# A four-layer network on one core: table loads in the planner's costs, a feature bias per 128 tokens, and a layernorm split off

## The chip, the core and the metric

The kernel runs on one core of a Trainium2 chip. The core has five engines, each with a queue of its own that it works through in order: PE (TensorE, matrix products), DVE (VectorE), ACT (ScalarE, activation functions), POOL (GpSimd), and SP (SyncE, which here only starts transfers). They wait for each other by semaphores. The metric is the device time of one execution in microseconds (us); less is better.

## The reference

2048 tokens of 128 features pass through four transformer layers, each an attention and a network, each behind a layernorm and added to the stream `x`. All data are fp32.

```python
x = x + L0_attn(ln(x))     # 16 heads of 64, softmax over all keys
x = x + L0_ffn(ln(x))      # 8 experts, top 1, capacity T/8
x = x + L1_attn(ln(x))     # 16 heads, causal
x = x + L1_ffn(ln(x))      # mixing with the token before, see below
x = x + L2_attn(ln(x))     # reduces to one 128x128 product
x = x + L2_ffn(ln(x))      # ternary weights, relu
x = x + L3_attn(ln(x))     # 16 heads, region mask, feature bias
x = x + L3_ffn(ln(x))      # binarised weights, gelu
```

Two parts matter here. The mixing (L1_ffn), for normed x with `x_prev` the same rows one token earlier:

```python
xr = mu_r * x + (1.0 - mu_r) * x_prev
xk = mu_k * x + (1.0 - mu_k) * x_prev
r = sigmoid(xr @ W_r);  k_act = square(relu(xk @ W_k))
out = r * (k_act @ W_v)
```

The feature bias of L3_attn, one number for each query token and head:

```python
hmid = gelu(x @ ext_w1 + ext_b1)                  # 5 features of 64
feature_scores = sigmoid(hmid . ext_w2 + ext_b2)  # 5 per token
bias = feature_scores @ softmax(faw).T            # [token, head]
attn = softmax(dots + bias)                       # bias along the query only
```

## The kernel before

The stream `x` stays on the chip for the whole run. A turned copy of its normed rows, `xT`, feeds the products. An attention layer runs over 8 pairs of heads; within a pair over 8 groups of 256 queries. For a group, PE makes scores in strips of 32 queries (L498), DVE moves each strip out of PSUM and takes row minima (`scan`, L508; the scores are made with the opposite sign), POOL and ACT gather the minima and hand them out as a shift (L554 to L568; in L3 POOL takes the bias off and adds it again on the way, L561 and L562), ACT does the exponentials (L580), DVE turns the result (L607), PE weighs the values (L639) and projects (L697), ACT divides (L707), POOL adds to `x` (L725).

Nothing of this is ordered by hand. Every piece of work is a `Step` with an engine, an estimated cost in us, what it comes after, and which buffers it takes. `run` (from L119) is a list scheduler: it simulates the five engines with the estimated costs and, again and again, gives out the step that can start first. On each engine the key (a tick, then the place) sets the preference; a later step goes ahead of a preferred one that still has to wait if, by the estimate, it ends within 0.1 us of the time at which that one can start (L147). The order in which the steps are given out is the order of the instructions in each engine's queue; at run time no engine passes over an instruction that waits. So an estimated cost changes no instruction, but it can change every queue behind it. Before the change a step has one fixed cost; some costs carry a part for loading activation tables, such as 2.6 for the sigmoids (L1147, L1239) and 1.9 for the first Gelu of a chunk (L1225). ACT holds one set of function tables at a time; the exponential, the sigmoid and the Gelu of this kernel are in different sets, and the compiler puts an ACT_TABLE_LOAD where the order changes from one to another.

Buffers come from rings. `MISC` is a ring of three PSUM banks (named `t` in the profile), used by almost everything but scores and weighing; `MID`, `MIXED` and `PAIRED` are rings of four, three and two SBUF tiles. A step that takes a buffer waits for the readers of the one that it replaces.

Between the first (L1) and the last (L3) of the attention layers that matter here lie, for each of five spans of tokens (three of 512, two of 256): the mixing (`rest`: a layernorm, the inputs xk and xr on ACT and DVE, L1096 to L1101, products L1130, L1105 and L1109, sigmoid L1147), a layernorm and the one product of L2's attention (`attend`, L1113), a layernorm and the ternary network (`feed_forward`, products L981 and L1003), and a layernorm for L3. Then for each chunk of 512 tokens the keys, queries and values of L3 (L392, L413) and the feature bias (`features`): three products and Gelus (L1220, L1225), a product and the sigmoid (L1233, L1239), and the weighing of the five features for 16 heads. L3 needs the keys of all tokens for its first scores.

The bias is wanted per strip: POOL reads `bias[0:Q]` (Q is 32) for the 32 queries of a strip, while DVE's minima sit on 128 partitions. In `features` before, POOL copies each strip of the scores four times side by side (L1247), one matmul makes the bias of one strip on all 128 partitions (L1254, 16 in a chunk), and DVE copies the result of four strips at a time (L1260). `bias` has 128 partitions, of which the readers use the first 32.

A layernorm (`normalise`, from L236) is statistics on DVE (L243 to L245), a power on POOL (L248 to L250), the scaling spread over ACT (L253), POOL or DVE (L258), a turn on PE (L264) and a copy on ACT (L279). The column of `xT` of the last token of a span is kept in `edge` (L1117) for the span behind it, in two columns used by turns, so that a new one waits for the readers of the old one.

Of the kernel before, what the change touches and what calls it, by code (L numbers as in the profile page):

```python
# [16 lines left out]
P = 128  # L17
# [41 lines left out]
def network(ctx: ExitStack, tc: tile.TileContext, a: dict, out: bass.AP):  # L59
# [18 lines left out]
    class Ring:  # L78


        def __init__(self, pool, name, shape, bufs, ordered=True):
            self.bufs, self.takers, self.held, self.ordered = bufs, [], [], ordered
            self.make = lambda: pool.tile(list(shape), F32, tag=name, name=name, bufs=bufs)
            rings.append(self)

    class Held:


        def __init__(self, ring):
            self.ring, self.users = ring, []  # L90

    class Step:
        def __init__(self, key, engine, us, do, after=(), takes=(), uses=(), then=None):
            self.key, self.engine, self.us, self.do, self.takes = key + (len(steps),), engine, us, do, takes
            self.after, self.order, self.then, self.end = list(after), [], then, None
            for h in takes:
                h.by = self
                h.users.append(self)
                h.ring.takers.append(self)
            for h in uses:  # L100
                self.after.append(h.by)
                h.users.append(self)
            steps.append(self)
# [15 lines left out]
    def run():  # L119
# [14 lines left out]
        open_, free, next_ = [[] for _ in range(5)], [0.0] * 5, [None] * 5  # L134
        for s in steps:
            if not s.left:
                open_[s.engine].append(s)
        for _ in range(len(steps)):
            best = None
            for e in range(5):  # L140
                found = None
                for s in [next_[e]] if next_[e] else sorted(open_[e], key=lambda s: s.key):
# [4 lines left out]
                    if found is None or t + s.us <= found[0] + 0.1:  # L147
# [8 lines left out]
            s.end = free[e] = start + s.us  # L156
            for h in s.takes:
                h.t = h.ring.make()
# [77 lines left out]
    def normalise(add, t0, n, after, before=(), row=None, hurry=False):  # L236


        mv, xn, pt = Held(MEANS), Held(NORMED), Held(MISC)
# [128 lines left out]
    class Pair:  # L368
# [19 lines left out]
        def projected(self, add, c, to, which, s, takes):  # L388
            pp, b = Held(MISC), self.layer.biases[which]
# [18 lines left out]
        def valued(self, add, c):  # L408
            pv, v = Held(MISC), self.v[c]
# [7 lines left out]
            made = add(PE, 0.8, make, self.layer.ready[c], takes=[pv, v], uses=[self.w])  # L417
# [19 lines left out]
    class Group:  # L437
# [104 lines left out]
        def spread_lowest(self, add, add_later, j, found):  # L542
# [16 lines left out]
            def with_bias():  # L559
                to, b = first().rearrange("p (h i) -> p h i", h=2), self.biases(j)[0:Q]  # L560
# [15 lines left out]
        def exps(self, add, j, h, part, shifted):  # L576
# [15 lines left out]
            return add(ACT, us, do, [shifted], takes=[self.sums] if first else [], uses=uses)  # L592
# [60 lines left out]
        def sum_up(self, add, made):  # L653

            ps, r = Held(MISC), Held(SHARES)
# [32 lines left out]
        def project_out(self, tick, weighed, r):  # L688

            y, pair, oT = [Held(MISC) for h in range(2)], self.pair, self.oT  # L690
# [88 lines left out]
    def output_bias(add):  # L779
        wo, pr = Held(DOUBLE), Held(MISC)  # L780
# [27 lines left out]
    def folded(add):  # L808
        q2T, av = [Held(MID) for k in range(4)], Held(MID)
        pb, pa, pt, pw = (Held(MISC) for k in range(4))  # L810
# [44 lines left out]
    moe_w = Held(DOUBLE)  # L855
# [4 lines left out]
    def experts(add, t0, after):  # L860

        r, pl, pc, pp, pb, pickT = Held(ROUTES), Held(MISC), Held(MISC), Held(MISC), Held(MISC), Held(PAIRED)
# [60 lines left out]
        made = add(ACT, 0.25, lambda: nc.scalar.activation(at(PROBS), at(PROBS), AF.Exp), [made], uses=[r])  # L923
# [10 lines left out]
        for i in range(4):  # L934
            pe, parts = [Held(MISC) for half in range(2)], Held(PAIRED)
# [37 lines left out]
    def feed_forward(add, t0, n, after, full, w1T, b1, func, w2T):  # L973

        hT, made, po = [Held(MID) for f in range(NC)], [], Held(MISC)
        for f in range(0, NC, 2):
            ph = [Held(MISC) for k in range(2)]
# [17 lines left out]
            for k in range(2):  # L995
                made.append(
                    add(ACT, wide(P * n), lambda k=k, f=f, ph=ph: act(f + k, ph[k]), uses=[ph[k], hT[f + k]])
# [14 lines left out]
        add(PE, 0.55 * n, second, made, takes=[po], uses=hT)  # L1012
# [8 lines left out]
    edge = keep([P, 2], "edge")  # L1021
    rests = [keep([P, 1], n) for n in ("rest_r", "rest_k")]
    ternary_w = Held(DOUBLE)

    def ternary(add):
# [14 lines left out]
        for i in range(2):  # L1040
            tot, g, half, less = (keep([P, 1], f"{n}{i}") for n in ("tot", "g", "half", "less"))
            pg, low = Held(MISC), Held(MID)
# [44 lines left out]
    edges = []  # L1087

    def rest(add, t0, n, after, hurry, made):
        m = P * n  # L1090
        xr, xk, ka, r = Held(MIXED), Held(MIXED), Held(MIXED), Held(PAIRED)
        pk, pr, pv, po = (Held(MISC) for k in range(4))
        xs, own = x[:, t0 : t0 + n, :], len(edges) % 2

        def parts(to, part):
            nc.scalar.mul(to.t[:, 1:m], xT[:, bass.ds(PAD + P * t0, m - 1)], part)  # L1096
            before = edge[:, 1 - own : 2 - own] if t0 else xT[:, PAD - 1 : PAD]
# [13 lines left out]
        def attend():  # L1111
            for i in range(n):
                nc.tensor.matmul(pv2.t[:, bass.ts(i, P)], lhsT=xT[:, cols(t0 + i)], rhs=w2, start=True, stop=True)  # L1113

        done, _ = normalise(add, t0, n, after, L1_read(t0, n), hurry=hurry)
        kept = add(
            DVE, 0.15, lambda: nc.vector.tensor_copy(edge[:, own : own + 1], xT[:, bass.ds(PAD + P * (t0 + n) - 1, 1)]),  # L1117
            [done] + (edge_read[-1] if edge_read else []),
        )
        read, mixed = [kept], []  # L1120
        for to, part, mu in ((xk, rests[1], mu_k), (xr, rests[0], mu_r)):
            s = add(ACT, 0.3 + wide(m), lambda to=to, part=part: parts(to, part), [done] + edges[-1:] + made, takes=[to])
            mixed.append(add(DVE, 0.1 + 0.00125 * m, lambda to=to, mu=mu: mix(to, mu), [s], uses=[to]))
            read += [s, mixed[-1]]
        edge_read.append(read[1::2])
        edges.append(kept)
# [9 lines left out]
        add(PE, 0.2 * n, receive, mixed[1:2], takes=[pr, r], uses=[xr])  # L1136
# [9 lines left out]
            2.6 + wide(m),  # L1146
            lambda: nc.scalar.activation(r.t[:, 0:m], pr.t[:, 0:m], AF.Sigmoid),  # L1147
            uses=[pr, r],
        )
        add(PE, 0.2 * n, gate, [square], takes=[pv], uses=[ka])  # L1150
# [17 lines left out]
        pv2 = po  # L1168
        attended = add(PE, 0.2 * n, attend, [done, w2_made], takes=[po])
# [16 lines left out]
    edge_read, bu_added, ob_added = [], [], [[] for c in range(4)]  # L1186

    def L1_read(t0, n):
        return L1.readers[t0 // 4]
# [3 lines left out]
    bias = keep([P, T // Q, H], "bias")  # L1193
# [3 lines left out]
    def feature_weights(add):  # L1197

        pf = Held(MISC)
# [7 lines left out]
        made = add(ACT, 0.25, lambda: nc.scalar.activation(fw, faw, AF.Exp, bias=fw_top), [made])  # L1207
# [4 lines left out]
    def features(add, c):  # L1212

        hm, made = [Held(MID) for j in range(3)], []
        fs, pf = Held(MIXED), Held(MISC)
        for j in range(3):
            n, ph = P if j < 2 else DH, Held(MISC)
# [10 lines left out]
            made.append(add(ACT, 0.6 if j else 1.9, act, uses=[ph, hm[j]]))  # L1228

        def score():  # L1230
# [6 lines left out]
        add(PE, 1.85, score, made, takes=[pf, fs], uses=hm)  # L1237
        scored = add(
            ACT, 2.6, lambda: nc.scalar.activation(fs.t[0:NF, :], pf.t[0:NF, :], AF.Sigmoid, bias=eb2),  # L1239
            uses=[pf, fs],  # L1240
        )
        for k in range(4):
            some, pbias = Held(PAIRED), Held(MISC)

            def spread(k=k, some=some):
                strips = fs.t[0:NF, :].rearrange("p (g q) -> p g q", q=Q)[:, 4 * k : 4 * k + 4, :]
                nc.gpsimd.tensor_copy(  # L1247
                    some.t[0:NF, :].rearrange("p (g c q) -> p g c q", c=4, q=Q),
                    strips.unsqueeze(2).to_broadcast([NF, 4, 4, Q]),
                )  # L1250

            def weigh(some=some, pbias=pbias):
                for i in range(4):
                    nc.tensor.matmul(  # L1254
                        pbias.t[:, bass.ts(i, H)], lhsT=some.t[0:NF, bass.ts(i, P)], rhs=fwT, start=True, stop=True
                    )

            def copy(k=k, pbias=pbias):
                to = bias[:, bass.ds(16 * c + 4 * k, 4), :].rearrange("p t h -> p (t h)")
                nc.vector.tensor_copy(to, pbias.t[:, 0 : 4 * H])  # L1260

# [173 lines left out]
```

## Time and profile before

| | us |
|---|---|
| median of 3 runs (3492.92 to 3493.73) | 3493.64 |
| the profiled execution | 3494.28 |
| its span, first to last instruction | 3492.6 |
| PE busy | 3397.9 (97%) |
| DVE busy | 3211.9 (92%) |
| ACT busy | 2807.6 (80%) |
| POOL busy | 965.4 (28%) |

The profile shows one execution. The times of the text are us from the start of its span. A matmul in fp32 shows up as two records, so 64 matmuls are 128. A line such as L1254 is a line of the kernel before.

The rows of the page for the parts that the change touches give, before a bar, the busy us and the mean ns of one, and after it the idle time of the engine just before, with what ended it:

```profile
L580 ACT ACT_TABLE_LOAD x10 | 12.8, 1283 | 0.2
L990 ACT ACT_TABLE_LOAD x5 | 6.4, 1283 | 0.1
L1225 ACT ACT_TABLE_LOAD x4 | 5.1, 1283 | 8.5 <-PE t L1220 6.5 <-issue 1.9
L1239 ACT ACT_TABLE_LOAD x4 | 5.1, 1283 | 0.1
L1147 ACT ACT_TABLE_LOAD x3 | 3.8, 1283 | 0.1
```

With one at the very start there are 27 table loads, 27 times 1283 ns or 34.6 us of ACT. The rows of the bias are 128 records of L1254 on PE (21.3 us busy), 16 copies of L1247 on POOL (9.5 us) and 16 of L1260 on DVE (3.3 us).

### The profile page before, as it was taken

The page shows a single profiled execution, that of the slowest core. Times are in us where ns is not written, and L with a number is a line of the kernel's source. Part 1 is how long each engine was busy: PE and PEld are TensorE (multiplying, and loading weights), DVE is VectorE, ACT ScalarE, POOL GpSimd, SP SyncE. Part 2 cuts the span into 40 slices and gives each one's busy share as a digit, 9 for nine tenths or more (in the row PEclk, how much of TensorE's full clock was granted, in tenths as well). Part 3 has the DMA queues.
Part 4 walks back from the last instruction along what each step waited for, and adds up shares of the span by engine and source line. Part 5 has one row for each costly group of instructions (what it writes and reads, how often), then busy time and mean ns, then how long its engine had stood idle before and what let it go on. Part 6 is the DMA issues. An engine that isn't in the chain of part 4 may idle for free. (4 is left out here: it accounts for less than half of the span.)

```text
span 3492.6 us, 115619 instructions
## 1 busy us (share of the span) xinstructions
PE 3397.9 (97%) x47018; PEld 1844.2 (53%) x47018; DVE 3211.9 (92%) x8019; ACT 2807.6 (80%) x8709; POOL 965.4 (28%) x2837
## 2 busy tenths in 40 slices
PE   8999999999999899999999988899999999999998
PEld 3545454554545455655555654455555555555555
DVE  8999999999999889989999883699999999999996
ACT  6888888888888667888888975578888888888886
POOL 2122222212222353232323344222222222222233
PEclk9999999999999899999999998899999999999999
DMA  1000000000000000000000000000000000000000
GB/s 47 2 5 2 5 5 2 5 2 5 5 2 5 1 5 8 6 6 6 6 6 6 6 2 4 4 5 5 2 5 2 5 4 4 5 2 2 2 5 10
DMA packets 22961, 19.00 MB, mean 5 GB/s; under 512 B 3556, under 2 KB 21612, under 8 KB 22426
## 3 DMA queue, kind: packets, MB, share of 16 engines
q1 hardware_dynamic: 22362, 11.55, 1.2%
q8 instruction: 368, 6.03, 0.7%
q14 instruction: 167, 1.37, 0.1%
q0 software_dynamic: 64, 0.06, 0.0%
HBM read 10.60 MB, written 1.05 MB: 3 GB/s over the span
## 5 line engine op out<-in xcount | busy, mean ns | idle before, releaser
L580 ACT ACTIVATE e<-e,shift 128x512 f32<-128x512 f32 (+14 forms) x3072 | 1973.9, 648 | 28.2 <-POOL shift L568 20.1
L508 DVE TENSOR_SCALAR_CACHE_REDUCE e<-s 128x512 f32<-128x512 f32 (+15 forms) x3072 | 1659.0, 589 | 99.5 <-PE s L498 98.5
L498 PE MATMUL s<-kT,qT 64*32 64x512 f32 (+8 forms) x24576 | 1458.4, 534 | 22.3 <-DVE e L508 22.3
L607 DVE STREAM_TRANSPOSE e<-e 128x2048 f32<-128x2048 f32 (+10 forms) x768 | 1435.2, 1871 | 9.3 <-ACT e L580 8.9
L639 PE MATMUL o<-e,v 128*64 128x256 f32 (+1 forms) x10496 | 1270.2, 374 | 6.1 <-DVE e L607 4.3
L639 PEld LDWEIGHTS o<-e,v 128*64 128x64 f32 x10496 | 748.3, 137 | 545.3 <-issue 297.7
L498 PEld LDWEIGHTS s<-kT,qT 64*32 64x32 f32 x24576 | 416.5, 105 | 518.8 <-issue 215.9
L580 ACT ACTIVATION_READ_ACCUMULATOR e<-e,shift 128x1 f32 x3072 | 591.3, 192 | 0.0
L554 POOL COPY low<-low 32x8 f32<-32x8 f32 x1152 | 211.3, 183 | 1182.6 <-DVE e L508 1144.1
L725 POOL TENSOR_TENSOR x<-x,part 128x256 f32<-128x256 f32 x384 | 281.1, 732 | 267.0 <-ACT part L707 251.7
L568 ACT COPY shift<-shift 32x8 f32<-32x8 f32 x768 | 149.9, 195 | 140.9 <-POOL shift L562 88.8
L707 ACT ACTIVATE part<-t,r 128x128 f32<-128x128 f32 x768 | 218.2, 367 | 43.9 <-PE t L697 36.2
L508 DVE DVE_READ_ACCUMULATOR e<-s 128x1 f32 x3072 | 230.9, 75 | 0.0
L392 PE MATMUL t<-xT,w 128*128 128x512 f32 x384 | 213.6, 647 | 3.7 <-ACT xT L279 3.5
L680 POOL TENSOR_TENSOR r<-r,inverse 128x4 f32<-128x4 f32 x128 | 130.5, 1020 | 304.4 <-ACT r L683 303.7
L712 ACT COPY oT<-o 128x256 f32<-128x256 f32 x192 | 70.7, 368 | 162.2 <-PE o L639 162.1
L639 PE MATMUL o<-e,va 128*64 128x128 f32 x1024 | 195.5, 273 | 0.0
L498 PE MATMUL s<-beyond,eye 64*32 64x32 bf16 x2560 | 159.9, 176 | 0.0
L697 PE MATMUL t<-w,oT 64*128 64x128 f32 x1536 | 139.8, 299 | 0.5 <-ACT xT L279 0.3
L697 PEld LDWEIGHTS t<-w,oT 64*128 64x128 f32 x1536 | 102.3, 187 | 67.9 <-issue 24.6
L639 PEld LDWEIGHTS o<-e,va 128*64 128x64 f32 x1024 | 126.0, 137 | 0.0
L498 PEld LDWEIGHTS <-regions 64*32 64x32 bf16 x1024 | 65.6, 93 | 113.4 <-issue 79.4
(187 smaller groups left out, 2107.3 us busy)
## 6 DMA issues: line engine op xcount, KB each, us to landing
w<-in_L_wq SPq DMA_DIRECT2D x24, 64.0 KB, 1.9
w<-in_L_wk SPq DMA_DIRECT2D x24, 64.0 KB, 2.2
w<-in_L_wv SPq DMA_DIRECT2D x24, 64.0 KB, 2.0
w<-in_L_wo SPq DMA_DIRECT2D x24, 64.0 KB, 2.1
x<-in_x SPq DMA_DIRECT2D x4, 256.0 KB, 4.7
out_x<-x SPq DMA_DIRECT2D x3, 256.0 KB, 2.3
big<-in_L_wo SPq DMA_DIRECT2D x1, 512.0 KB
big<-in_moe_w SPq DMA_DIRECT2D x1, 512.0 KB
```

The source lines that it names most:

```text
L392: nc.tensor.matmul(pp.t, lhsT=self.w.t[:, which, :], rhs=xT[:, cols(4 * c, 4)], start=True, stop=True)
L498: nc.tensor.matmul(s[h].t[on, bass.ds(first, size)], lhsT=lhsT, rhs=rhs, start=m == 0, stop=m == len(terms) - 1,)
L508: nc.vector.tensor_scalar(self.e(h)[:, i, 0:n], s.t[:, 0:n], 1.0, None, ALU.mult, ALU.min, accum_out=self.lows[j].t[:, 0, 4 * h + i % 4 : ...
L554: nc.gpsimd.tensor_copy(low.t[0:Q, c], low.t[bass.ts(c, Q), 0])
L568: (nc.gpsimd.tensor_copy if causal else nc.scalar.copy)(shift.t[bass.ts(c, Q)], first())
L580: nc.scalar.activation(e, e, AF.Exp, bias=self.shifts[j].t[:, 4 * h + i % 4 : 4 * h + i % 4 + 1], scale=-1.0, accum_out=self.sums.t[:, h, ...
L607: nc.vector.transpose(rows()[:, :, 0:n], rows()[:, :, 0:n])
L639: nc.tensor.matmul(self.o.t[bass.ds(DH * h, DH), i0:i1, :], lhsT=lhsT, rhs=self.e(h)[:, i0:i1, bass.ts(t, Q)], start=t == 0, stop=t == las ...
L680: nc.gpsimd.tensor_tensor(some, some, inverse, ALU.pow)
L697: nc.tensor.matmul(y[h].t[:, bass.ts(j, P)], lhsT=oT.t[half, bass.ts(j, P)], rhs=pair.w.t[half, 3, :], start=True, stop=True,)
L707: nc.scalar.mul(part.t[:, j, :], y[h].t[:, bass.ts(j, P)], r.t[:, j, h : h + 1])
L725: POOL, 0.74, lambda part=part: nc.gpsimd.tensor_tensor(xs, xs, part.t, ALU.add), [divided], uses=[part]
```

## The change

Three things. The planner keeps the set of tables that ACT would hold and adds 1.3 us to a step that needs another one (`us(s)`); the steps with Exp, Sigmoid and Gelu say which they need, and the parts for tables leave their fixed costs. With this, some other costs are set anew (values 0.8 to 1.0, blocks of 128 in the mixing 0.2 to 0.26, the second product of a network 0.55 to 0.93 per block, `score` 1.85 to 2.8). The feature bias is made for 128 tokens in one matmul, with the tokens on the partitions, and four copies bring the four strips to the first 32 partitions; POOL's copies and 12 of 16 matmuls of a chunk are gone. The mixing's first layernorm is added as steps of its own, all five ahead of the rest, and each span has its own column of `edge`. Tiles also get names of their own in the profile (a product of the bias is `pbias` now, not `t`).

```diff
+        table = None
+
+        def us(s):
+            return s.us + (1.3 if s.table and s.table != table else 0.0)
...
-                    if found is None or t + s.us <= found[0] + 0.1:
+                    if found is None or t + us(s) <= found[0] + 0.1:
...
-            s.end = free[e] = start + s.us
+            s.end = free[e] = start + us(s)
+            table = s.table or table
...
-            made = add(PE, 0.8, make, self.layer.ready[c], takes=[pv, v], uses=[self.w])
+            made = add(PE, 1.0, make, self.layer.ready[c], takes=[pv, v], uses=[self.w])
...
-            return add(ACT, us, do, [shifted], takes=[self.sums] if first else [], uses=uses)
+            return add(ACT, us, do, [shifted], takes=[self.sums] if first else [], uses=uses, table=AF.Exp)
...
-        add(PE, 0.55 * n, second, made, takes=[po], uses=hT)
+        add(PE, 0.93 * n, second, made, takes=[po], uses=hT)
...
-    edge = keep([P, 2], "edge")
+    edge = keep([P, NT], "edge")
...
+    def first_norm(add, t0, n, after, hurry):
+        done, _ = normalise(add, t0, n, after, L1.readers[t0 // 4], hurry=hurry)
+        last = t0 + n - 1
+        to, some = edge[:, last : last + 1], xT[:, bass.ds(PAD + P * (t0 + n) - 1, 1)]
+        kept[t0 + n] = add(DVE, 0.15, lambda: nc.vector.tensor_copy(to, some), [done])
+        return done
...
-        done, _ = normalise(add, t0, n, after, L1_read(t0, n), hurry=hurry)
-        kept = add(
-            DVE, 0.15, lambda: nc.vector.tensor_copy(edge[:, own : own + 1], xT[:, bass.ds(PAD + P * (t0 + n) - 1, 1)]),
-            [done] + (edge_read[-1] if edge_read else []),
-        )
-        read, mixed = [kept], []
+        read, mixed = [kept[t0 + n]], []
+        needs = [done] + made + ([kept[t0]] if t0 else [])
...
-            2.6 + wide(m),
+            wide(m),
             lambda: nc.scalar.activation(r.t[:, 0:m], pr.t[:, 0:m], AF.Sigmoid),
             uses=[pr, r],
-        )
-        add(PE, 0.2 * n, gate, [square], takes=[pv], uses=[ka])
+            table=AF.Sigmoid,
+        )
+        add(PE, 0.26 * n, gate, [square], takes=[pv], uses=[ka])
...
-    bias = keep([P, T // Q, H], "bias")
+    bias = keep([Q, T // Q, H], "bias")
...
-            made.append(add(ACT, 0.6 if j else 1.9, act, uses=[ph, hm[j]]))
+            made.append(add(ACT, 0.6, act, uses=[ph, hm[j]], table=AF.Gelu))
...
-        add(PE, 1.85, score, made, takes=[pf, fs], uses=hm)
+        def weigh():
+            for i in range(4):
+                nc.tensor.matmul(
+                    pbias.t[:, bass.ts(i, H)], lhsT=fs.t[0:NF, bass.ts(i, P)], rhs=fwT, start=True, stop=True
+                )
+
+        def copy():
+            for q in range(4):
+                to = bias[:, bass.ts(c, 16), :].rearrange("p (t i) h -> p i t h", i=4)[:, q]
+                nc.vector.tensor_copy(to, pbias.t[bass.ts(q, Q), 0 : 4 * H].rearrange("p (t h) -> p t h", h=H))
+
+        add(PE, 2.8, score, made, takes=[pf, fs], uses=hm)
         scored = add(
-            ACT, 2.6, lambda: nc.scalar.activation(fs.t[0:NF, :], pf.t[0:NF, :], AF.Sigmoid, bias=eb2),
-            uses=[pf, fs],
-        )
-        for k in range(4):
-            some, pbias = Held(PAIRED), Held(MISC)
-
-            def spread(k=k, some=some):
-                strips = fs.t[0:NF, :].rearrange("p (g q) -> p g q", q=Q)[:, 4 * k : 4 * k + 4, :]
-                nc.gpsimd.tensor_copy(
-                    some.t[0:NF, :].rearrange("p (g c q) -> p g c q", c=4, q=Q),
-                    strips.unsqueeze(2).to_broadcast([NF, 4, 4, Q]),
-                )
...
-            made = add(POOL, 0.6, spread, [scored], takes=[some], uses=[fs])
-            add(PE, 0.8, weigh, [made, fwT_made], takes=[pbias], uses=[some])
-            L3.biased[c].append(add(DVE, 0.16, copy, uses=[pbias]))
+            ACT, 0.6, lambda: nc.scalar.activation(fs.t[0:NF, :], pf.t[0:NF, :], AF.Sigmoid, bias=eb2), uses=[pf, fs],
+            table=AF.Sigmoid,
+        )
+        add(PE, 0.7, weigh, [scored, fwT_made], takes=[pbias], uses=[fs])
+        L3.biased[c].append(add(DVE, 0.5, copy, uses=[pbias]))
...
+    mix_spans = [(0, 4), (4, 4), (8, 4), (12, 2), (14, 2)]
     spans = [(0, 4), (4, 4), (8, 4), (12, 2), (14, 2)]
...
-    for t0, n in spans:
-        rest(planner(L1.left(t0, n)), t0, n, L1.outputs(t0, n) + [bu_added[t0 // 4]], n < 4, made)
+    done = {}
+    for t0, n in mix_spans:
+        done[t0] = first_norm(
+            planner(L1.left(t0, n)), t0, n, L1.outputs(t0, n) + [bu_added[t0 // 4]], n < 4
+        )
+    for t0, n in mix_spans:
+        rest(planner(L1.left(t0, n)), t0, n, done[t0], n < 4, made)
```

## The prediction

> **What bounds the kernel now.** I cut the span where the character of the work changes and read the windows view of these stretches (columns: busy us of PE, PE's weight loads, DVE, ACT, POOL, then granted clock, DMA share, GB/s):
>
> ```profile
> 1400.00:2000.00 600.00, 593.01 (x11755) 358.09 (x11746) 544.66 (x1977) 512.48 (x1931) 184.86 (x706) 1.00 0.02 6
> 2000.00:2150.70 150.70, 132.40 (x1468) 81.35 (x1467) 108.56 (x338) 107.01 (x292) 68.07 (x141) 0.91 0.01 2
> 2150.70:2230.60 79.90, 60.06 (x248) 38.91 (x250) 22.98 (x94) 32.29 (x66) 25.73 (x46) 0.81 0.02 7
> 2230.60:2270.40 39.80, 35.30 (x429) 14.48 (x429) 38.01 (x93) 29.17 (x80) 10.39 (x43) 0.87 0.01 2
> 2270.40:3370.00 1099.60, 1098.85 (x14662) 588.63 (x14670) 1076.04 (x2253) 908.23 (x2702) 283.46 (x873) 1.00 0.01 3
> ```
>
> In the attention layers PE has no gap to speak of (593 of 600, 1098.9 of 1099.6): there a microsecond of PE work is a microsecond of time, and work of the other engines is free while it fits. At 2230 to 2270, where the third attention layer (L3) opens, DVE is the bound (38.0 of 39.8). The change works mostly in 2000 to 2230, the mixing and the ternary network. PE is busy 132 of 151 us at a clock of 0.91 while the attention layer before (L1) ends, and 60 of 80 us at 0.81 in the tail behind its last weighing (the last L639 of L1 ends at 2150.7; the first scores of L3 start at 2230.6). No engine is full in the tail; it is one chain from token span to token span. So I read the chain of waits there, in order of time (start us, us, what):
>
> ```profile
> 2129.89 6.56 PE t L1254 x32
> 2136.46 2.01 PE t L1130 x2
> ...
> 2181.53 2.08 PE t L392 x2
> 2183.61 6.93 PE t L1254 x32
> 2190.54 1.15 PE t L1130 x2
> ...
> 2275.47 0.99 PE t L1254 x8
> ...
> 2289.94 3.80 PE t L1254 x32
> ```
>
> L1254 is `weigh`, the feature bias; each fp32 matmul is recorded as two, so 16 matmuls of a chunk are 32 records. All four chunks show up on PE, and two full batches stand on the path of the stretch that has no other bound.
>
> **The feature bias, per 128 tokens.** It removes, per chunk of 512 tokens, 4 POOL spreads and 12 of 16 matmuls with a 128x16 result; the 4 DVE copies of 64 elements a partition remain, on 32 partitions (now 211 ns each, and I keep that: free in either form). The spreads, 16 of 604 ns, 9.5 us, cost nothing now: POOL is busy 28% of the span, and PE was always late enough for them. The matmuls I price by batch.
> (a) Chunk 0: 6.56/32 = 205 ns a record. 8 records are 1.64 us: **-4.9 us**. Next late would be L1130, whose input was mixed by 2126.0, and the last weighing of L1, whose last transpose ended at 2131.6: both were ready inside the batch, so PE passes the gain on.
> (b) Chunk 1: 6.93 to 1.73 us, -5.2. The L1130 behind it had its input from the mix at 2177.89 (0.49 us) and only queued. The changed order issues the two receiving matmuls (L1105, 0.85 us) ahead of the bias, in a gap; but ACT now makes both mixing inputs before the sigmoid, 0.8 us later for the x transpose. **-5.3 us**.
> (c) Chunks 2 and 3: 24 records of chunk 2 ran at 2245, while DVE was the bound: nothing. The other 0.99 us and the 3.80 of chunk 3 lie where PE is the bound again. The 8 records that chunk 3 keeps are 0.95 at 119 ns: **-3.8 us**. Two of its three L1220 matmuls also move ahead to where DVE is the bound, up to -1.9 more, which I leave for the range.
>
> Here a rule is weighed. The Trainium skill, "TensorE: Matmul & The Clock Gate", Part 1 (the HAM clock gate), lets PE reach full clock after some 3.4 us of sustained work. The trace of PE in 4 us windows (busy us, clock) disagrees for this batch:
>
> ```profile
> 2184.00:2188.00 4.00, 4.00 (x20) 0.50 0.00 0
> 2188.00:2192.00 4.00, 4.00 (x17) 0.50 0.01 4
> ```
>
> Busy throughout, half clock throughout; the same at 2132 to 2140. By the rule 17 of the records would take 3.4 us and 15 some 1.8 at 119 ns, and (b) would save 3.5, not 5.2. I take the row. The rule also speaks against the change: less PE work, more cold time. Against that, matmuls behind the batch were cold already (L1130 of 256 columns 1.15 us there, 0.69 at 2197.97); (a) and (b) together lie between -7 (the rule, twice 3.5) and -14 (8 records at 119 ns each, 5.6 and 6.0, and some 2 us of warmer matmuls behind).
>
> **The planner's table loads.** No instruction is added by it directly; costs of steps change, and with them the order. Compared engine by engine, SP's order is the same; L0 and most of L3 differ only in small swaps. The number of table loads does not fall: 27 before, 30 after. The planner charges 1.3 to the step that switches, but a step that fills a gap is not charged for switching Exp back in. The places:
> - End of L1 and tail: one load more before the last weighing. ACT is busy 107 of 151 us; I charge it in full, **+1.3 us**.
> - Opening of L3: the three Gelus of chunk 3 stand singly among exponentials, each with a load there and back: 4 loads more, 5.1 us. ACT idles 10.6 of 39.8 us there, and the transposes run up to 5 us behind the exponentials they wait for. Nothing; without that cover, +5.1.
> - The last network (L990): two loads fewer, in its second of five spans, where they stand on the chain:
>
> ```profile
> 3418.84 1.28 ACT L990
> 3420.14 1.27 ACT mid L990 x2
> 3421.42 1.28 ACT L580
> 3422.72 1.52 ACT e L580 x4
> 3424.26 1.28 ACT L990
> 3425.55 0.70 ACT mid L990
> 3426.25 0.04 issue
> 3426.29 3.84 PE t L1003 x32
> ```
>
> 2.6 us of ACT leave, but PE stood for only 1.5 of the 10 us from 3420, and DVE has its gap too: between 0 and -2.6, **-2 us**.
>
> The price of a load is the second rule. The skill, "ScalarE: Activation LUTs", section What ACT_TABLE_LOAD costs, has 1283 ns plus a drain, some 2.66 us a switch, and its advice is to finish one set before another. The trace has the first part alone: the load at 2179.04 takes 1.28 us and its sigmoid starts at 2180.34, so 1.30 in all. Three loads more are 3.9 us of ACT by the row, 8.0 by the page; the row decides, and the planner's 1.3 is right for one switch.
>
> Other costs in the plan (0.8 to 1.0 for the values, 0.2 to 0.26 a block, 0.55 to 0.93 for the second layer) come nearer to the rows (16 records of L1003 take about 1.9 us warm), so the plan should fit better. What order does by itself the trace of before cannot show. Bounds: PE's idle time in 2000 to 2150.7, 18.3 us, is the most to be won, and a like loss is possible; no row favours either, and I take 0.
>
> **The first layernorm as a step of its own.** Same instructions, same priority (its ticks follow L1's last groups in either form). It drops one wait, of the copied edge column for readers of the old one. In the trace L1117 waited 5.7 us in all, for its own xT copy (L279): **0**. Behind it on DVE stand copies and statistics that go no earlier.
>
> Sum: -4.9 - 5.3 - 3.8 + 1.3 - 2.0 = -14.7 us. The profiled execution took 3494.28 (span 3492.6, 1.7 around it), 0.64 above the median of 3493.64. 3494.3 - 14.7 = **3479.6 us**.
>
> **The rivals.**
> 1. *The better plan closes gaps as well* (0.23): half of the 18.3 us goes. For it: the changed order starts the second span's network some 8 exponentials earlier against the end of L1, and those of the old costs that were furthest off belong to this stretch. Against: PE's rows there also wait on layernorm chains (POOL waited 67.9 us for statistics in 2000 to 2230). 3479.6 - 9.2 = 3470.4.
> 2. *The batch was cover, not cause* (0.19): without it PE waits for the next layernorm. (a) goes wholly and half of (b): -14.7 + 4.9 + 2.6 = -7.2, 3487.1. For it: 0.75 PE density in the tail. Against: the inputs behind each batch were ready.
> 3. *ACT blocks PE, slower* (0.06). Gelus and sigmoids that fill gaps stand in ACT's queue ahead of the divisions (L707) that free PSUM slots. The trace has the case: before the batch of chunk 0, PE stood 3.1 us for an L707 behind a sigmoid and its two loads. The changed order has 22 loads from the mixing to L3's opening against 17. 14.7/3.1: from 5 such stalls on the gain is gone; 8 would give 3479.6 + 24.9 = 3504.5. Against: the planner sees PSUM slots and ACT's order, and the single Gelus sit where ACT has gaps.
> That the change doesn't do what it says is half true already (more loads, not fewer), and is in the sum.
>
> **How the numbers follow.** My forecast has 0.52. Down, rival 1 with the -1.9 of (c) and warmer clocks reaches 3464; up, rival 2 with 3 us of worse order reaches 3490: range 3464 to 3490; its remainder is below 0.2. A measurement here tells 0.2%, 7 us, from no change. Below 3486.6 lie nearly all of my forecast, rival 1 and under half of rival 2: faster 0.82; the rest of rival 2 and a little of the forecast: same 0.13; slower 0.05.
>
> **What would show it.** In the changed profile: 32 records of the bias matmuls, not 128, no POOL spread; the tail from the last L1 weighing to the first L3 score near 74.5 us, not 79.9; 30 table loads; L3's middle unchanged in pace; the second span of the last network without a load inside. I am wrong if the tail stays near 80 (rival 2), if PE idles clearly less or more than 18 us before the last weighing (rivals 1 and 3), or if the expert stretch, 1150 to 1400, where only order changes, moves by more than 4 us.

## The result and the profile after

The changed kernel takes **3463.44 us** (median of six runs, 3461.14 to 3471.93); the kernel before took 3493.22 beside it (six runs, 3492.4 to 3493.73). The ratio is 0.992, with a 95% interval of 0.9908 to 0.9933. The direction was as forecast, the gain of 30 us twice the forecast 14.7, and the time lies 0.6 us under the lower end of the range. The profiled execution took 3463.54, its span 3461.8 (before: 3494.28 and 3492.6). PE is busy 3378.0 us (98%), DVE 3211.7, ACT 2810.9, POOL 951.3: PE lost 20 us of work and POOL 14; ACT gained 3, its added table loads.

To see where the time went I take an instruction that every kernel issues equally often and always in the same order, the `scan` of DVE (3072 of them), and compare the start of the k-th one in both executions. The differences between neighbouring marks say what each stretch gained or lost:

| stretch (us of the kernel before) | forecast | measured |
|---|---|---|
| start to 1986 | 0 | -4.7 |
| to the last weighing of L1 (2150.7) | -4.9 (chunk 0), +1.3 (load) | -13.3 |
| tail, to the first scores of L3 (2230.6) | -5.3 (chunk 1) | -11.6 |
| opening of L3, to 2312 | -3.8 | -5.1 |
| middle of L3, to 3285 | 0 | +4.0 |
| last network, to the end | -2.0 | 0.0 |
| sum | -14.7 | -30.7 |

The first four rows, 34.7 us, hold all of the gain; in the middle of L3 a part is given back. The first row is not clear of chance: two kernels of the experiments with the same order of instructions there, layernorm_as_before and binary_spread, stand at +2.5 and -3.6 in it. The windows view of the changed kernel, cut at the same places of its work (columns: busy us of PE, its weight loads, DVE, ACT, POOL, then the granted clock, DMA share, GB/s):

```profile
1995.30:2132.80 137.50, 127.07 (x1445) 74.10 (x1444) 107.75 (x338) 107.00 (x292) 63.89 (x135) 0.95 0.01 2
2132.80:2201.04 68.24, 49.93 (x222) 29.76 (x227) 23.13 (x94) 32.57 (x68) 25.21 (x44) 0.87 0.03 9
2201.04:2240.80 39.76, 35.15 (x420) 13.78 (x420) 37.97 (x92) 32.52 (x77) 7.95 (x39) 0.88 0.01 1
```

The first row, the end of L1, starts 4.7 us earlier than the 2000 of the kernel before, since that much was won by then. In it PE's idle time is 137.5 - 127.1 = 10.4 us where it was 18.3, PE is busy for 5.3 us less, near the 5.5 that the bias of chunk 0 saves, and the clock is 0.95 where it was 0.91. In the second, the tail, PE is busy 49.9 us where it was 60.1, at 0.87 and not 0.81: of the 11.6 us won there 10.1 are PE's busy time, and its idle time has hardly moved (19.8 to 18.3). The third row starts 29.6 us earlier and is as long as it was.

The chain of waits shows the new batches of the bias (start us, us, what):

```profile
2104.51 1.07 PE pbias L1248 x8
...
2163.18 0.69 ACT fs L1259
2163.91 1.06 PE pbias L1248 x8
2164.97 1.07 PE pp L399 x2
```

L1248 is the bias product now. Chunk 0 takes 1.07 us for 6.56, chunk 1 1.06 for 6.93, so 133 ns a record; I had taken 205. The key product behind chunk 1 (`pp`, two records of 512 columns) takes 1.07 us. The like product just ahead of the old batch took 2.08: half clock had begun with it (2181.5) and lasted 13.7 us, through the whole batch; no half clock is left at this place.

The page has 32 records of the bias, no copy on POOL, and 30 table loads, the largest groups of them these:

```profile
L587 ACT ACT_TABLE_LOAD x12 | 15.4, 1283 | 0.2
L1234 ACT ACT_TABLE_LOAD x6 | 7.7, 1283 | 7.1 <-PE ph L1229 6.6 <-issue 0.5
```

L587 is the exponential (10 loads before, at L580), L1234 the Gelu of the features (4 before).

### The profile page after: what moved, and what is told of

It reads as the page before. It is cut to its first block, busy times and chain, and to the rows that moved or that the text cites. A ratio compares the mean times of both kernels' runs of the same rounds, so it can differ in the third digit from the quotient of the medians.

```text
span 3461.8 us, 115408 instructions
## 1 busy us (share of the span) xinstructions
PE 3378.0 (98%) x46922; PEld 1819.8 (53%) x46922; DVE 3211.7 (93%) x8019; ACT 2810.9 (81%) x8712; POOL 951.3 (27%) x2821
## 4 chain that ended last, share of the span: by engine, by line
PE 82%; DVE 11%; ACT 4%; issue 2%; POOL 1%; DMA 0%; SPq 0%; POOLq 0%; DVEq 0%; ACTq 0%
PE s L505 33%; PE o L646 32%; DVE e L515 5%; PE pp L399 5%; DVE e L614 3%; PE y L704 3%; PE pv L420 3%; ACT e L587 2%; PE t L622 2%; PE ps L667 1%; PE pe L947 1%; PE ph L989 1%; PE po L1014 1%; PE pt L271 0%; DVE st L250 0%
## 5 line engine op out<-in xcount | busy, mean ns | idle before, releaser
L587 ACT ACTIVATE e<-e,shift 128x512 f32<-128x512 f32 (+14 forms) x3072 | 1973.7, 649 | 26.3 <-POOL shift L575 18.6
L505 PE MATMUL s<-kT,qT 64*32 64x512 f32 (+8 forms) x24576 | 1463.3, 535 | 20.6 <-DVE e L515 20.5
L505 PEld LDWEIGHTS s<-kT,qT 64*32 64x32 f32 x24576 | 417.0, 105 | 518.2 <-issue 220.6
L587 ACT ACTIVATION_READ_ACCUMULATOR e<-e,shift 128x1 f32 x3072 | 591.9, 193 | 0.0
L714 ACT ACTIVATE part<-y,r 128x128 f32<-128x128 f32 x768 | 217.6, 366 | 38.7 <-PE y L704 36.9
L399 PE MATMUL pp<-xT,w 128*128 128x512 f32 x384 | 213.7, 646 | 0.7 <-ACT xT L286 0.7
L505 PE MATMUL s<-beyond,eye 64*32 64x32 bf16 x2560 | 160.0, 177 | 0.0
L704 PE MATMUL y<-w,oT 64*128 64x128 f32 x1536 | 139.0, 297 | 0.9 <-DVE bias L1255 0.4
L704 PEld LDWEIGHTS y<-w,oT 64*128 64x128 f32 x1536 | 101.6, 186 | 67.1 <-issue 23.6
L505 PEld LDWEIGHTS <-regions 64*32 64x32 bf16 x1024 | 66.3, 93 | 117.3 <-issue 84.1
```

The source lines that it names most:

```text
L399: nc.tensor.matmul(pp.t, lhsT=self.w.t[:, which, :], rhs=xT[:, cols(4 * c, 4)], start=True, stop=True)
L505: nc.tensor.matmul(s[h].t[on, bass.ds(first, size)], lhsT=lhsT, rhs=rhs, start=m == 0, stop=m == len(terms) - 1,)
L587: nc.scalar.activation(e, e, AF.Exp, bias=self.shifts[j].t[:, 4 * h + i % 4 : 4 * h + i % 4 + 1], scale=-1.0, accum_out=self.sums.t[:, h, ...
L704: nc.tensor.matmul(y[h].t[:, bass.ts(j, P)], lhsT=oT.t[half, bass.ts(j, P)], rhs=pair.w.t[half, 3, :], start=True, stop=True,)
L714: nc.scalar.mul(part.t[:, j, :], y[h].t[:, bass.ts(j, P)], r.t[:, j, h : h + 1])
```

## The experiments

My theory after the result: the bias is worth about what its own terms say, and the rest comes from the order that the new costs give. The rivals: the batches alone explain all of it, through the clock of what stands behind them; or the split layernorm does. Two kernels change the batch in an order that stays fixed, seven take the parts one by one and together, three go after a single place. All times are medians, ratios against the kernel before, whose runs beside them stayed near 3493 us.

### The batch alone, the order fixed

`before_4matmuls` is the kernel before, with one product for four strips; the costs stay, so the order does.

```diff
-                for i in range(4):
-                    nc.tensor.matmul(
-                        pbias.t[:, bass.ts(i, H)], lhsT=some.t[0:NF, bass.ts(i, P)], rhs=fwT, start=True, stop=True
-                    )
+                nc.tensor.matmul(
+                    pbias.t[:, 0 : 4 * H].rearrange("p (i h) -> p i h", h=H),
+                    lhsT=some.t[0:NF, 0:P],
+                    rhs=fwT.unsqueeze(1).to_broadcast([NF, 4, H]),
...
```

> The kernel before with its order of instructions kept, but in the feature bias 4 matmuls of 64 columns a chunk in place of 16 of 16 columns (the bias of every strip is then that of the first of its four strips: this part of the computation is changed). The planner is told nothing. Theory A (the batches themselves were on the path): 5.0 us for chunk 0, 5.2 for chunk 1 and 3.8 at L3's opening go, 3493.2 - 14 = 3479. Theory B (the time came from the order, the batches were cover): at most half, 3486 or more.

Measured 3483.81 us, ratio 0.9973 (0.9962 to 0.9984); by stretches -7.2 in the mixing and tail, -1.6 in the opening of L3 and just behind it, nothing in its middle. The gain of 9.2 us lies between the two theories (14, or at most half of it). The chain of waits of this kernel:

```profile
2130.61 0.55 POOL mid L1247
2131.20 1.24 PE t L1253 x4
...
2179.50 1.05 PE t L1253 x4
2180.58 0.24 DVE bias L1263
2180.84 1.24 PE t L1253 x4
```

Ahead of the last four records of chunk 0 now stands POOL's spread (L1247), and in chunk 1 a copy of DVE that gives back a PSUM bank. Chunk 0's batch fell only to 3.3 us, chunk 1's to 2.6. I had costed the spreads at nothing because PE was always late enough for them; that cover was the batch itself. In the real change the spreads go as well, so the sum isn't wrong by it.

`after_16matmuls` is the changed kernel with every bias product made four times over.

```diff
-            for i in range(4):
+            for i in [0, 1, 2, 3] * 4:
```

> The changed kernel with its order kept, but each of the 4 bias matmuls of a chunk made four times over (16, as before). The trace of after has 1.06 us for a batch of 8 records, so 32 records are 4.2 us at that clock. Theory A: the batches of chunks 0 and 1 return in full, 3.2 each, and 1 to 3 at L3's opening, so 7 to 9 us slower than after (3463.4), 3471 to 3473; up to 14 if the clock falls to half. Theory B: under 4 us slower.

Measured 3484.66 us, ratio 0.9977 (0.9969 to 0.9985): 21 us lost, far more than expected. Of this the mixing and tail lose 13.0 by the scans and L3's opening 7.7. The chain:

```profile
2105.63 3.84 PE pbias L1248 x32
...
2170.16 6.65 PE pbias L1248 x32
2176.81 2.01 PE pp L399 x2
...
2229.51 4.64 PE pbias L1248 x32
```

Of the four batches, 1.06 to 1.07 us each in the change, three are 3.84, 6.65 and 4.64, and the fourth takes 5.13 us in the trace: 16 us more in all. The product behind the second one is back at 2.01 us. Summing the windows of half clock in 1950 to 2300 of the trace gives 44 us for the changed kernel and 68 for this one (72 for the kernel before). So the batch costs twice: its own length, 16 of the 21 us, and the clock of what stands behind it, to which I put down most of the other 5; how these divide was not measured apart. The same 96 records are worth 21 us in the new order; in the old one, with the spreads left in place, they were worth 9.

### The parts, one by one and together

Three parts can be put in or left out: the count of table loads (T), the feature bias (B), the other costs (C). The edits are those of the diff above; for T, and for C:

```diff
             return s.us
+            return s.us + (1.3 if s.table and s.table != table else 0.0)
...
-            2.6 + wide(m),
+            wide(m),
```

```diff
-            made = add(PE, 0.8, make, self.layer.ready[c], takes=[pv, v], uses=[self.w])
+            made = add(PE, 1.0, make, self.layer.ready[c], takes=[pv, v], uses=[self.w])
...
-        add(PE, 0.55 * n, second, made, takes=[po], uses=hT)
+        add(PE, 0.93 * n, second, made, takes=[po], uses=hT)
```

> The kernel before with the planner's table count alone (bias, other costs and layernorm as before; 25 table loads, not 27). If the order by the table count made the larger part of the 15 us that the prediction did not foresee: 3475 to 3480. If it did not: within 4 us of 3493.

> The kernel before with the bias per 128 tokens alone (31 table loads). Theory A: 14 us less by the matmuls, plus or minus the new order, 3479; four more table loads stand in L3's opening and cost nothing. Theory B: 3486 or more, the gain is in the other parts.

> The kernel before with the other re-set costs alone (values 1.0, blocks 0.26, second product 0.93, score 2.8). If the parts add up, tables +19.7 and bias -14.8 leave -34 for these costs: 3459. If a new order is worth what it happens to be worth, the parts don't add, and this lies anywhere within 20 us of 3493.

> Tables and other costs, bias as before. If the parts add: 3463.4 + 14.8 = 3478. If the costs are needed for the table count to be worth anything (tables alone, PE's steps were still planned too short): also clearly below 3493. If orders are as good as chance: anywhere in 3475 to 3515.

> Tables and bias, other costs as before. If the parts add: 3493 + 19.7 - 14.8 = 3498. If the loss of tables alone came from where the 16-matmul batch stood in that order, it goes with the batch: 3480 or less.

> Bias and other costs, the table loads in fixed costs as before (32 loads). If the parts add: 3463.4 - 19.7 = 3444. If the planner's table count carries the gain of the whole change: 3475 or more.

The last of them has all three parts and only the layernorm of the mixing as it was, a part of `rest` again:

> The changed kernel with the mixing's first layernorm in one piece with the rest, as before. Its order differs from after in places of the edge copies on DVE alone. If that part is worth nothing: 3463 within 3. If the wait of the edge column mattered: 3 to 6 more.

Measured (us; the stretches are differences to the kernel before by the scans, as above; the opening of L3, -6.8 to +3.6, and its middle, -2.2 to +4.0, make up the rest):

| kernel | median | ratio, 95% | start to 1986 | mixing, tail | last network |
|---|---|---|---|---|---|
| T, tables_alone | 3512.66 | 1.0055 (1.004 to 1.007) | +3.4 | +6.3 | +5.6 |
| B, bias_alone | 3478.13 | 0.9958 (0.9941 to 0.9975) | -2.6 | -10.0 | -1.3 |
| C, costs_alone | 3493.64 | 1.0003 (0.9994 to 1.0011) | -5.3 | -6.7 | +12.0 |
| TC, tables_and_costs | 3478.96 | 0.9961 (0.9946 to 0.9975) | -4.0 | -12.3 | +1.3 |
| TB, tables_and_bias | 3495.6 | 1.0008 (0.9999 to 1.0017) | +3.4 | -3.2 | +5.4 |
| BC, bias_and_costs | 3486.97 | 0.9984 (0.9977 to 0.9991) | -5.3 | -13.3 | +13.8 |
| TBC, layernorm_as_before | 3470.32 | 0.9933 (0.9918 to 0.9948) | +2.5 | -24.8 | 0.0 |
| the change | 3463.44 | 0.992 (0.9908 to 0.9933) | -4.7 | -24.9 | 0.0 |

Three things follow. **The bias alone** brings 15.1 us, what its terms summed to (14.0); it brings 17.1 on top of T, but only 6.7 on top of C, and 8.6 (TBC) to 15.5 (the change) on top of both. **The count of table loads alone loses 19.4 us**, and the other costs alone win nothing, yet together they win 14.3. Neither is good or bad by itself. The parts do not add: a sum would have put C at 3459 and BC at 3444, and T lies outside both values that I had given it. On top of the bias the two together are worth 7.8 (TBC) to 14.7 (the change). **The split layernorm**: TBC and the change agree within 0.2 us in every stretch but one, 1250 to 1415, where TBC has 7.0 us more. The order of the instructions is the same there; TBC meets 24 us of half clock in it, the change 10. The six runs of the change themselves fall into 3461 to 3464 (four) and 3470 to 3472 (two); of TBC's four, three lie at 3470 and one at 3465. So the split is worth nothing that I can tell from this scatter, and some 7 of the 30 us may be the luck of which group the median fell into.

Why T and C need each other can be read at three places.

*At the start.* Kernels with T but the old costs lose some 12 us between scans 48 and 64 (3 of them won just before). The windows view of tables_alone there:

```profile
80.00:85.00 5.00, 2.91 (x40) 0.62 (x32) 4.75 (x10) 4.92 (x16) 0.26 (x2) 1.00 0.00 0
85.00:90.00 5.00, 3.25 (x40) 0.66 (x32) 5.00 (x11) 5.00 (x15) 0.28 (x2) 0.90 0.00 0
90.00:95.00 5.00, 5.00 (x44) 2.48 (x34) 5.00 (x10) 4.21 (x14) 1.55 (x4) 0.50 0.01 3
```

DVE and ACT are full and PE, with only scores in its queue, stands for DVE (three waits, 5.1 us); after that its clock falls to 0.50 for a window of 5 us. In the changed kernel PE is busy 5.00 of 5 us in the first two of these windows.

*At the end of L1.* The mark here is the product that closes the mixing of the third span (`gate`), against the last weighing of L1:

| kernel | gate of the third span | last weighing of L1 ends | first scores of L3 | tail |
|---|---|---|---|---|
| before | 2141.1 | 2150.7 | 2230.6 | 79.9 |
| T | 2151.1 | 2146.6 | 2240.3 | 93.7 |
| TB | 2149.2 | 2144.7 | 2230.9 | 86.2 |
| B | 2135.6 | 2145.2 | 2218.0 | 72.8 |
| C | 2130.3 | 2134.9 | 2218.6 | 83.7 |
| TC | 2126.4 | 2134.9 | 2214.4 | 79.4 |
| BC | 2129.2 | 2135.1 | 2212.1 | 77.0 |
| the change | 2125.3 | 2132.8 | 2201.0 | 68.2 |

In the kernel before the gate stands 9.6 us ahead of that end. With T and the old costs the mixing of this span comes 4.5 us after the last weighing, when PE has nothing else left to lay beside its layernorms. In the 20 us from 2150, tables_alone shows PE busy for 5.02 us at a clock of 0.60. With C the last weighing ends at 2133 to 2135 in every case of the table, 10 to 13 us sooner beyond what was won by 1986. The windows view of bias_alone and of tables_and_costs, from the place of the work that is 2000 in the kernel before to the last weighing, shows where that comes from:

```profile
1997.40:2145.20 147.80, 129.60 (x1444) 76.75 (x1442) 108.43 (x338) 106.87 (x291) 66.21 (x137) 0.91 0.01 2
1996.00:2134.90 138.90, 131.24 (x1469) 78.96 (x1467) 107.80 (x338) 108.08 (x293) 66.76 (x140) 0.93 0.01 2
```

The bias alone leaves PE's idle time at 18.2 us (18.3 before); with the costs and the count, and the old bias, it is 7.7, and in the four kernels of the table with C it is 7.7 to 12.2. So the order closes these gaps and the bias does not. But C alone lengthens the tail. With T and C both, the gate comes 7.5 to 8.5 us ahead of that end, and with the bias as well the tail is short.

*In the last network.* C without T loses 11 us between scans 3008 and 3024 and wins 4 back by 3040. The chain of costs_alone there, and then that of the changed kernel at the same work:

```profile
3369.93 1.28 ACT L998
3371.22 1.27 ACT hT L998 x2
3372.54 6.42 PE po L1014 x32
```

```profile
3349.00 2.91 PE s L505 x25
...
3356.18 3.79 PE po L1014 x32
```

In both kernels, and in the one before, two exponentials stand between the two pairs of Gelus of the first span, with a load there and a load back (a row of 1.28 us without a tile's name is a load). So it isn't this split that costs the 11 us. What differs is PE's work meanwhile. In the changed kernel 7.2 us of scores (L505) stand ahead of the second product (L1014), which then starts without a wait. In costs_alone these scores stand behind it: PE waits 3.1 us for the Gelus, half clock is granted from 3371.2 for 6.8 us, and the product takes 6.42 us for 3.79. bias_and_costs loses 10.8 us at the same scans and shows the same (6.33 us), while tables_and_costs, which differs from costs_alone by the count alone, has PE busy without a gap in the 8 us ahead of the product. This is what the count is good for here: a planner that charges the two loads sees the Gelus come later, and lays other work ahead of the product that waits for them. In the second span T and C together also leave out two loads. The number of loads says little: it is 27 before, 28 with C, 25 with T, 26 with both, and 29 to 32 with the bias.

### One cost of the six

Of the six values of C, is the second product's 0.93 the one that T needs? `table_bias_second_0.93` has T, B, the split layernorm and this one value:

```diff
-        add(PE, 0.55 * n, second, made, takes=[po], uses=hT)
+        add(PE, 0.93 * n, second, made, takes=[po], uses=hT)
```

> Tables and bias, and of the other costs only the second product at 0.93 a block. Against tables_and_bias (3495.6) the order is the same up to the mixing. If the two re-set parts correct each other by place: the 8.6 us lost at the start stay (they hang on the values' 1.0), the 7.6 us lost in the last network go, the mixing gains too: 3475 to 3488. If the gain is chance of order: no better than 3495.

Measured 3476.82 us, ratio 0.9953 (0.9938 to 0.9968), 18.8 less than TB. In the mixing it brings -3.2 to -20.5: the gate of the third span is back 6.3 us ahead of the last weighing (2134.4 against 2140.6), and the tail is 71.9. At the start the loss between scans 48 and 64 stays (10.0 us); of the costs of C, only that of the values (1.0) belongs to a step that runs there, which makes it, by elimination, the one that mends this place. In the last network the value did little (7.6 us lost behind the last scan in TB, 5.7 here), against what I had expected.

### What the middle of L3 gives back

The weights of the last network are binarised by small steps on DVE. In the kernel before they lay at 2287 to 2319, 2422 and 2834; in the changed order three of the ten come at 2257 to 2265 and the other seven as one block. The chain of the changed kernel:

```profile
2798.69 0.19 DVE low L1289
...
2806.24 0.70 DVE w L1291
...
2807.08 0.63 PE pw L1301 x4
```

The windows view of it (columns as above):

```profile
2800.00:2810.00 10.00, 7.44 (x73) 4.37 (x73) 9.62 (x26) 3.86 (x10) 1.82 (x4) 0.92 0.00 1
```

DVE is taken for 8 us, no scan runs, PE drains (7.44 of 10) and ACT too (3.86). The scans show 4.9 us lost at this place. `binary_spread` gives each block of these steps a tick of its own, six apart; `binary_spread_load_back` lets the planner count a table load twice as well when it fills a gap, for the way back.

```diff
+        tick = L3.begin + 128
...
+                add_part = planner(tick)
+                tick += 6
...
-                    if found is None or t + us(s) <= found[0] + 0.1:
+                    if found is None or t + 2 * us(s) - s.us <= found[0] + 0.1:
```

> The changed kernel, with the ten DVE steps that binarise the last weights at five ticks, 6 apart, and not all at one. After shows them in one run of 8 us at 2798.7, and the distance to before shrinks by 5.4 us there. If that bunch costs them: 3458. If something else does: 3463.

> As binary_spread, and a step that fills a gap is also charged for the load of the set that it displaces. 29 loads in place of 30. If loads in L3's opening are covered, as the prediction has it: as binary_spread, within 2 us. If they cost what they take: 1.3 to 5 us less.

Measured 3469.12 us (0.993, 0.9915 to 0.9945) and 3467.75 (0.9925, 0.9908 to 0.9942): the medians show no gain on the change. The scans say more. At the old place both win 3.3 us on the kernel before, where the change lost 4.9, and they lose 4.8 between 2890 and 2925, where these steps stand now, partly in two blocks on DVE's chain. Over the whole middle of L3 they lose 1.5 us where the change lost 4.0. So the spreading wins 2.5 us in its own stretch, and most of the work is not hidden, only moved. That the median of binary_spread is higher all the same comes from elsewhere: its order is that of the change up to 2312, and yet it stands there at -20.9 for -24.9 in the mixing and tail and at -2.7 for -5.1 in the opening of L3, with 27 us of half clock in the tail for 17. The same order is worth 4 us more or less by the clock that it meets. The second kernel has 29 loads for 30, and no stretch in which that shows.

## Why the prediction was right in its sign and half in its size

**The feature bias was right in sum.** Alone it brings 15.1 us against the 14.0 of (a), (b) and (c). By place, the mixing and tail took 10.0 of the 10.2 forecast for (a) and (b), and the opening of L3 3.5 for 3.8. That the sum fits so well is in part luck: 2.9 came before the last weighing for the 4.9 of (a), and 7.1 in the tail for the 5.3 of (b), and 2.6 were won before 1986, where the order is that of the kernel before. The price of a record was too high (133 ns measured for 205 taken), since the eight records no longer meet a half clock; that is 0.6 us a batch.

**The step that failed is the last one on the planner: "no row favours either, and I take 0".** The order is worth 14.3 us without the bias and 7.8 to 14.7 with it. Rival 1 is what came true beside the forecast. Its measure, PE's idle time before the last weighing, fell from 18.3 to 10.4, near the half that it took, and the bias alone leaves it at 18.2. Its time of 3470.4 lies 7 us above the result. Of these, 4.7 were won before the mixing, and 4.2 in the tail, where PE works at 0.87 for 0.81: there 24 records of the bias account for 5.9 of the 10.1 us that PE lost, and the other 4.2 are the same products in less time. Neither is clear of chance. In the same order layernorm_as_before stands at +2.5 before the mixing, and binary_spread's PE does the work of the tail at 0.81, in 53.5 us for 49.9; the medians of these two, 3470.32 and 3469.12, are what rival 1 gave. The signs against it were read wrongly: the layernorm chains that POOL waits for do stay, but what PE has to do beside them can be brought earlier.

A row did favour a gain. The sum noted that the old costs furthest off belonged to this stretch, and that 16 records of the second product take 1.9 us where the planner counted 1.1. It took this as a better fit in general, not as a place where an instruction stands too late. The table of the gates shows what it does where the count is in: 0.93 with the bias and the count moves the third span's mixing from 4.5 us behind the end of L1 to 6.3 ahead of it. Against the kernel before, whose gate was ahead already, what C brings is the smaller idle time before that end. Which of its values brings it was tried for 0.93 alone: with T, B and the split it is 11.5 us, where TB has 14.3.

**Rivals 2 and 3.** The batch was cause, not cover: the tail was to come to 74.5 and came to 68.2, where rival 2 had it near 80. In the old order, though, cutting it uncovered another wait, much as rival 2 had it, but for POOL's spreads and not for a layernorm: the batches fell to 3.3 and 2.6 us and not to 1.6 and 1.7. Rival 3, slower by a worse order, isn't the change's outcome, but it exists: the count alone costs 19.4 us. What these kernels show is not ACT blocking PE by divisions, the mechanism I gave, but PE without work in the tail (27.9 us idle with T, 19.8 before) and at the start.

**The smaller terms.** The loads in the opening of L3 stand on the chain of waits (the one at 2234.27, the Gelu behind it and the load back at 2236.91 follow each other there), and yet the stretch won 5.1 us, within the 3.8 to 5.7 given: cover enough. The -2.0 in the last network didn't come: its two stretches are +1.3 and -1.3, although the second span has no load inside, as forecast. The +1.3 for the load before the last weighing can't be told apart within the 13.3 won there. The middle of L3 was to keep its pace and lost 4.0, for steps that the diff doesn't touch. The expert stretch moved by 2.0 us, within the 4 allowed; but in layernorm_as_before, in the same order, it moved by 7.5, so this sign could not have told anything. The split layernorm was 0, as far as the scatter lets one see.

**The two rules that were weighed.** On the clock, the row was the better guide: the Trainium skill, "TensorE: Matmul & The Clock Gate", Part 1, would have the narrow batch warm after some 3.4 us of work, and in after_16matmuls 32 records took 6.65 us at a clock of 0.53, with PE busy throughout. But what I drew from it, that less PE work would mean more cold time, did not hold: half clock fell from 72 to 44 us in 1950 to 2300. On the load, where the Trainium skill ("ScalarE: Activation LUTs", What ACT_TABLE_LOAD costs) has some 2.66 us for a switch, the trace's 1.30 us held again: in costs_alone the Gelus start 1.29 and 1.30 us after their loads do.

**Open.** Why TBC meets more half clock than the change in 1250 to 1415, in the same order; whether the two groups of the change's runs are this same difference (only one run of each kernel has a profile); which of C's values closes PE's gaps before the last weighing, and which mends the last 5.7 us of the last network.

## What to carry to other kernels

A planner's costs hang together: one cost set right among wrong ones can lose 19 us, and the whole set win 14, so test them together, and look for the step that an order puts behind the end of a stage instead of ahead of it, or behind a wait instead of into it. Before a median is explained by an edit, compare the stretches in which the order did not change. A batch of narrow products is priced with what stands behind it, as the clock it leaves is paid by the next product too. When a batch goes, ask what it covered, and for small steps that no engine has room for, ask where a new order will heap them up.

## What the runs showed of the hardware

PE at work without a gap can stay at half clock: in after_16matmuls 32 records of 16 columns took 6.65 us in one place (208 ns each, clock 0.53) and 3.84 in another (120 ns) of the same kernel. Half clock comes in whole pieces: in all fourteen traces every stretch of it, but the one that the end of the trace cuts, lasts 3.4 us or two to seven times that. The same order of instructions can meet 10 us of half clock in one kernel and 24 us in another over the same 165 us of work, and come out 7.0 us apart; the kernel before, with six runs within 1.3 us, shows nothing of the kind. In tables_alone half clock came behind idle time: two windows with PE busy for 58% and 65% were followed by one at 0.50.
